# A message-passing kernel whose first table comes ahead of the check of dst, and whose last edges are cut into batches of 4, 4 and 1 tiles

## The chip, the core and the metric

The kernel runs on one core of a Trainium2 chip. A core has four compute engines, each with its own queue of instructions that it works off in order: TensorE (PE in the profile; PEld is its weight load), VectorE (DVE), ScalarE (ACT) and GpSimd (POOL). SyncE (SP) only issues DMAs here. Sixteen DMA engines move data between the chip's memory and the core's; SP and ScalarE feed one kind of queue (q1 and q10 in the profile), GpSimd another (q0). The metric is the device time of one execution in microseconds (us), lower is better.

## The reference

The graph has 1250 nodes with 512 values each and 40000 edges that are sorted by their target `dst`. One block of message passing is followed by a residual and a layer norm. Cut to what is computed:

```python
x_j = x[src]
v_j = x_j[:, :384].reshape(E, 128, 3)
s_j = silu(x_j[:, 384:] @ W1 + b1) @ W3 + b3
rbf = sqrt(2 / R_CUT) * sin(n * pi * r / R_CUT) / r          # n = 1..20, r = edge_weight
cutoff = 0.5 * (cos(pi * r / R_CUT) + 1) * (r < R_CUT)
s1, s2, s3 = thirds of s_j * (rbf * cutoff @ W2 + b2)
msg = concat([v_j * s1 + s3 * edge_attr, s2])
x1 = x + segment_sum(msg, dst)
x_j = x1[src]
v = x_j[:, :384].reshape(E, 3, 128) @ U ; v_V = v @ V
h = silu(concat([norm(v_V), x_j[:, 384:]]) @ Wu1 + bu1) @ Wu2 + bu2
s1, s2, s3 = thirds of h
msg = concat([v * s1, einsum(v, v_V) + s3])
out = layernorm(x + x1 + segment_sum(msg, dst))
```

## The kernel before

**What is computed per node instead of per edge.** `s_j` before the edge factor depends on the source node alone, so a first table of 10 blocks of 128 rows (L577, `table_row`) is written to memory once, and the edges gather rows of 640 values from it. The second message too depends on the source alone, so it is made once for each node, and the second segment sum becomes a product: `counts`, the number of edges from one node to another, times the rows of the second message. `counts` is gathered while the first message runs (`make_pair`, `mark_sources`, `count_links`).

**Tiling.** The edges are cut into 79 chunks of 512 (the last one holds 64), four chunks to a group, 20 groups. A batch is one tile of 128 edges from each of the four chunks of a group, so a group has four batches, and a batch is one step of the loop. The last group has three chunks, one with only 64 edges, so its batches have 3, 2, 2 and 2 tiles: 80 steps (`NT`). As `dst` is sorted, the edges of a chunk are expected to fall into a window of 32 target nodes that moves by 16 from chunk to chunk; L278 to L290 count the edges that do not (`missed`), and a branch at L383 takes `windowed` if there are none and `general` otherwise. With these inputs it is `windowed`.

**The front** (L126 to L385). The edge lists are loaded one chunk to a row by `load_edges` (L132): 78 full rows, and one more DMA for the 64 edges that are left. `dst` has a tile of its own; attributes, sources and weights lie in the memory of `counts`. SP issues in this order: dst, b3 and bu2, w1, b1, w3, weight, src, attributes, and later the ten stores of table rows. VectorE makes constants, then the check of `dst` (L278 to L290), then copies the transposed scalar part of the nodes (`turn_s`, L317). TensorE and ScalarE make the inner layer (`inner_layer`, L322 and L323), then each table row takes two matmuls (L336, L337), a ScalarE copy (L578), a VectorE product (L579) and a store on SP (L584). Between the rows the sources are turned (L344, L349), and behind them the second half of the bias is split into a high and a low part (`split_bias`, L360 to L365).

**The prologue of `windowed`** (L1458 to L1489). Weights and attributes are transposed (`by_tile`, L303 and L304, into `weight` and `carried`), VectorE makes `ratio` (L681), the arguments of the sines, `fade`, and the `basis` of the first group (L788), and then splits the sources (L699 to L721). ScalarE makes the sine (`turn`, L779). TensorE turns the basis (L800) and makes the edge factors `eb` of the first step (L854).

**The loop** (L1490). At each step VectorE makes the messages of a batch (`messages`: L812, L865, L883, L823, L869), TensorE adds those of the step before into the sums of a group (`add_messages`, L900 and L907) and counts its links (L925), then makes the edge factors of the next step into the one buffer `eb` (L854), which VectorE has to have read first. GpSimd gathers three steps ahead (`gather`, L745); the gathers are held behind `edge_factors` of the step by an explicit dependency. All other work is put into one of four lists, `first`, `early`, `late` and `dve`, by `at(when, step, rank, function)`, and runs at a fixed place of its step in order of rank:

```python
for t in range(max(*first, *early, *late, *dve) + 1):
    if t < NT:
        messages(t)
    run(first, t)
    if 1 <= t <= NT:
        add_messages(t - 1)
        count_links(t - 1)
    run(early, t)
    if t + 1 < NT:
        made = edge_factors(t + 1)
    if t + ahead < NT:
        gather(t + ahead, made)
    run(late, t)
    run(dve, t)
```

Such work is: closing a group (`close_group`, L938 to L951, the copies of the sums are L938 and L944), the counts (`low_counts` L960, `keep_counts` L969 and L974), and for each of ten blocks of nodes the sum of two groups (`sum_block`, L992, with a selection matrix `sel` that puts window rows to nodes), the nodes' own rows (`fetch_nodes` L999, `take_block` L1008), and the chain of the second message: `keep_rest` L1018, `turn_nodes` L1031, `times_u` L1042, `times_uv` L1058 with the squares L1062, `lengths` L1079, `root` L1096, `hidden` L1102, `curve` L1109, `factors` L1116 to L1132, `scale_row` L1138, `dot_row` L1147, `end_row` L1155 to L1164, `part_row` L1177. Block 8 takes sums of groups 16 and 17, block 9 those of 18 and 19.

**The tail.** Behind the messages the products of counts and rows (`products`, L1248) that were not made in the loop are made, the sums that were spilled are fetched and added on GpSimd (`add_begun`, L1221), the last counts are cast (`cast_counts`, L1231), and each block is added, normalised and stored (`end_out` L1279 to L1285, `norm_out` L1291 to L1303; the ten are done in `order`). The dependency on `ended` at L1236 keeps casts behind the last row of block 9.

Of the kernel before, what the change touches and what calls it, by code (L numbers as in the profile page):

```python
# [21 lines left out]
P = 128  # L22
C = 128
# [16 lines left out]
MARGIN = 8  # L40
WIN = SHARE + 2 * MARGIN
# [23 lines left out]
def gnn_resnorm(  # L65
# [63 lines left out]
    full = n_edges // CHUNK  # L129
    rest = n_edges - full * CHUNK  # L130

    def load_edges(t, ap, per=1):  # L132
# [10 lines left out]
    bias_f = front.tile([BIAS_ROWS - 1 + 32, V + 2 * C], F32, name="bias_f")  # L143
    nc.vector.memset(bias_f, 0.0)

    unfilled = full // 32 * 32
    nc.vector.memset(sh.att_r[unfilled:, :], 0.0)
# [8 lines left out]


    inside = SHARE * (NCP - 1) - MARGIN
    assert all(0 <= inside - (SHARE * c - MARGIN) < WIN for c in range(full, NCP))
    dst_r = front.tile([NCP, CHUNK], I32, name="dst_r")  # L160
    nc.gpsimd.memset(dst_r[unfilled:, :], inside)
    load_edges(dst_r, dst)
    first_last = slice(0, 3, 2)
    three = bias_f.rearrange("(r q) f -> r q f", q=32)[:, 0, :]
    nc.sync.dma_start(three[:, :V], b3.rearrange("(o f) -> o f", o=1).to_broadcast([3, V]))
    for h in range(2):
        nc.sync.dma_start(
            three[:, V + h * C : V + (h + 1) * C],
            bu2.rearrange("(h o c) -> h o c", o=1, c=C)[2 * h].to_broadcast([3, C]),
        )  # L170

    sh.nodes = const.tile([P, NB * width], F32, name="nodes")
    sh.xt = sh.nodes.rearrange("p (b f) -> p b f", f=width)
# [6 lines left out]
    last = n_nodes + MARGIN - (NB - 1) * P  # L180
    warm = const.tile([P, 1], F32, name="warm")
    nc.vector.memset(warm, 0.0)
    nc.vector.memset(sh.xt[last // 32 * 32 :, NB - 1, :], 0.0)
    nc.vector.memset(sh.xt[:MARGIN, 0, :], 0.0)

# [6 lines left out]
    load_all_nodes(nc.scalar, slice(V, width))  # L192

    nc.scalar.activation(warm, warm, AF.Silu)

    diff = front.tile([P, P], I32)
    nc.gpsimd.iota(diff, pattern=[[1, P]], base=0, channel_multiplier=-1)
    nc.gpsimd.memset(sh.src_r[unfilled:, :], 0.0)
# [6 lines left out]
    def load(engine, ap, shape, name):  # L205
        t = const.tile(shape, F32, name=name)
        engine.dma_start(t, ap)
        return t

    sh.h_t = const.tile([C, NB * P], F32, name="h_t")
# [1664 lines left out]
```

## Time and profile before

| | us |
|---|---|
| median of three runs | 591.55 |
| lowest and highest | 590.14, 593.16 |
| the profiled execution | 585.79 |
| its span, first to last instruction | 583.8 |

| engine | busy us | share |
|---|---|---|
| TensorE | 445.5 | 76% |
| VectorE | 441.8 | 76% |
| ScalarE | 373.6 | 64% |
| GpSimd | 354.5 | 61% |

The TensorE clock granted over the span is 0.888 of full speed. The profile is of one execution, so durations and waits in it add up to its own 583.8, not to the median. A line of a timeline is: start, duration, engine, line of the program, operation, the tile written and the one read, shapes, how often, and in brackets how long the engine was idle before and which instruction ended that.

Where the time lies: the first message starts at 41.04, a step of the loop takes some 6 to 6.5 from step 3 on, the last message ends at 539.77, and the last output is issued at 578.59. In the first 40 us the granted clock was 0.96 in 28 to 33 and 0.50 in 33 to 47.

### The profile page before, as it was taken

The numbers are of one execution on the slowest core, as the hardware profiler recorded it, in microseconds if no ns is written. First come the engines' busy times: TensorE is split into PE (matmuls) and PEld (weight loads), VectorE is DVE, ScalarE is ACT, GpSimd is POOL, SyncE is SP. The second block draws the span as 40 slices with busy tenths as digits, with TensorE's granted clock in tenths as the row PEclk, the third lists the DMA queues.
The fourth block names the chain that finished last, engine by engine and source line by source line (L and its number), as shares of the span: only waits on it lengthen the run. The fifth ranks groups of instructions, "written<-read, shape, count | busy, mean of one in ns | idle before, by whom it ended". The sixth has DMA issues, their size and how long they took to land. (4 is left out here: it accounts for less than half of the span.)

```text
span 583.8 us, 11028 instructions
## 1 busy us (share of the span) xinstructions
PE 445.5 (76%) x4193; PEld 240.2 (41%) x4193; DVE 441.8 (76%) x698; ACT 373.6 (64%) x941; POOL 354.5 (61%) x369
## 2 busy tenths in 40 slices
PE   2845667687777887697888786787777878798894
PEld 1422323344444344334435443443443444353673
DVE  7685867878878777878877777777787777687685
ACT  1455364757677665767776767777667778656455
POOL 7265767656667665656656665666666576643850
PEclk9966986888899777979888889998989899889998
DMA  8766777786777767767877777777777787859514
GB/s 240 257 189 213 200 224 216 210 262 200 216 224 243 228 197 218 214 205 220 253 245 201 253 226 213 233 231 242 220 229 224 218 240 224 241 148 285 210 38 146
DMA packets 38321, 126.95 MB, mean 217 GB/s; under 512 B 6688, under 2 KB 8238, under 8 KB 38258
## 3 DMA queue, kind: packets, MB, share of 16 engines
q0 software_dynamic: 26016, 104.86, 60.5%
q1 hardware_dynamic: 10910, 20.64, 10.2%
q10 hardware_dynamic: 1332, 0.64, 0.4%
q8 instruction: 35, 0.57, 0.4%
q14 instruction: 28, 0.23, 0.1%
HBM read 114.78 MB, written 11.34 MB: 216 GB/s over the span
## 5 line engine op out<-in xcount | busy, mean ns | idle before, releaser
L745 POOL DMA_INDIRECT more<-table,src_i x189 | 189.9, 1005 | 107.3 <-issue 44.0
L745 POOL DMA_INDIRECT nodes<-table,src_i x124 | 126.3, 1019 | 74.0 <-issue 28.3
L854 PE MATMUL eb<-w_sb,basis_t 25*128 25x388 f32 x626 | 83.5, 585 | 76.6 <-issue 42.2
L845 ACT ACTIVATE one<-one,weight,src_f 128x128 f16<-128x128 f16 x313 | 128.5, 482 | 0.5 <-issue 0.2
L835 ACT ACTIVATE one<-number,low 128x128 f16<-128x128 f16 x313 | 99.8, 392 | 8.5 <-PE adj L925 3.3
L812 DVE TENSOR_TENSOR hot<-lane,eb 128x128 f32<-128x128 f32 (+1 forms) x81 | 22.7, 281 | 81.6 <-PE eb L854 44.7
L869 DVE TENSOR_TENSOR more<-more,eb 128x1536 f32<-128x1536 f32 (+2 forms) x49 | 82.6, 1688 | 0.0
L854 PEld LDWEIGHTS eb<-w_sb,basis_t 25*128 25x128 f32 x626 | 27.5, 196 | 99.5 <-issue 58.0
L900 PE MATMUL agg<-more,hot 128*32 128x512 f32 (+1 forms) x378 | 66.0, 752 | 1.2 <-ACT sums L956 1.2
L865 DVE TENSOR_TENSOR more<-more,eb 128x1024 f32<-128x1024 f32 (+2 forms) x49 | 57.5, 1175 | 0.4 <-issue 0.3
L907 PEld LDWEIGHTS agg<-more,spread 128*32 128x32 f32 x1134 | 39.5, 125 | 40.8 <-issue 40.1
L869 DVE TENSOR_TENSOR nodes<-nodes,eb 128x1536 f32<-128x1536 f32 (+1 forms) x32 | 54.2, 1695 | 0.0
L907 PE MATMUL agg<-more,spread 128*32 128x128 f32 x1134 | 47.8, 298 | 0.0
L823 DVE TENSOR_TENSOR spread<-hot,eb 128x384 f32<-128x384 f32 (+1 forms) x81 | 43.0, 532 | 0.0
L925 PE MATMUL adj<-pair,one 128*128 128x160 f16 x313 | 37.9, 243 | 5.0 <-issue 4.9
L900 PE MATMUL agg<-nodes,hot 128*32 128x512 f32 x248 | 38.5, 680 | 2.4 <-ACT sums L956 2.4
L883 DVE TENSOR_TENSOR pair<-number,column 128x640 f16<-128x640 f16 (+1 forms) x81 | 38.5, 476 | 0.0
L805 ACT COPY basis_t<-work 128x512 f32<-128x512 f32 x20 | 11.7, 587 | 41.1 <-PE work L800 21.7
L865 DVE TENSOR_TENSOR nodes<-nodes,eb 128x1024 f32<-128x1024 f32 (+1 forms) x32 | 37.8, 1180 | 0.0
L960 DVE SCALAR_TENSOR_TENSOR both<-both,adj 128x400 f16<-128x400 f16 (+1 forms) x20 | 11.3, 566 | 32.0 <-ACT both L951 21.1
L907 PEld LDWEIGHTS agg<-nodes,spread 128*32 128x32 f32 x744 | 23.6, 116 | 23.1 <-issue 22.9
L925 PEld LDWEIGHTS <-one 128*128 128x128 f16 x313 | 20.8, 100 | 22.1 <-issue 20.7
(258 smaller groups left out, 728.8 us busy)
## 6 DMA issues: line engine op xcount, KB each, us to landing
table<-more SPq DMA_DIRECT2D x10, 320.0 KB
spilled<-begun SPq DMA_DIRECT2D x12, 256.0 KB
more<-table,src_i POOLq DMA_INDIRECT x189
more<-spilled SPq DMA_DIRECT2D x2, 1280.0 KB
resid<-h_t SPq DMA_DIRECT2D x9, 256.0 KB
node_x<-in_x_dram SPq DMA_DIRECT2D x8, 256.0 KB
nodes<-table,src_i POOLq DMA_INDIRECT x124
nodes<-in_x_dram POOLq DMA_DIRECT2D x2, 768.0 KB
```

The costliest lines, as they stand in the source:

```text
L745: got = nc.gpsimd.indirect_dma_start(out=rows_t[:n, j, :], out_offset=None, in_=sh.table1, in_offset=bass.IndirectOffsetOnAxis(ap=sh.src_i ...
L812: nc.vector.tensor_tensor(hots[t][:m, js, :], lane[:m, None, :WIN].to_broadcast(shape), eb[:m, js, V + 3 : V + 4].to_broadcast(shape), op= ...
L823: nc.vector.tensor_mul(spread[t][:m, js], hots[t][:m, js, None, :].to_broadcast(shape), eb[:m, js, V : V + 3, None].to_broadcast(shape),)
L835: nc.scalar.activation(onehots[t][:, j, :], number[:, :P], AF.Abs, bias=low[:, e : e + 1])
L845: nc.scalar.activation(one, one, AF.Relu, scale=less[:, e : e + 1], bias=worth[:, e : e + 1])
L854: made = nc.tensor.matmul(eb[:, j, : V + CARRY], turned[g][rows, i, :], sh.w2_sb[rows, :], start=True, stop=True,)
L865: nc.vector.tensor_mul(msg[:m, js, V:], msg[:m, js, V:], eb[:m, js, C:V])
L869: nc.vector.tensor_mul(msg[:m, js, :V].rearrange("p t (k c) -> p t k c", k=3), msg[:m, js, :V].rearrange("p t (k c) -> p t k c", k=3), eb[ ...
L883: nc.vector.tensor_tensor(pair[:m, js, :].rearrange("p t (l h) -> p t l h", h=2), number[:m, : PARTS * WIN].rearrange("p (l h) -> p l h", ...
L900: nc.tensor.matmul(agg[j * WIN : (j + 1) * WIN, :], hots[t][:m, j, :], msg[:m, j, :width], start=(i == 0), stop=False, skip_group_check=True,)
L907: nc.tensor.matmul(agg[j * WIN : (j + 1) * WIN, c * C : (c + 1) * C], spread[t][:m, j, c, :], msg[:m, j, width:], start=False, stop=(i == ...
L925: nc.tensor.matmul(to[:, :, at : at + WIN], one[:m, j, :], pair[:m, j, :].rearrange("e (p n) -> e p n", n=WIN), start=(i == 0 and j == js[ ...
```

## The change

*In the front* the loads are issued in another order (SP: w1, b1, b3, w3, dst, bu2, src, weight; the attributes only behind the ten stores of table rows). The copies of `turn_s` go from VectorE to ScalarE. The inner layer is cut into blocks (1, 2), (3, 4), (5 to 8), (0, 9), and the table rows of blocks 1 to 8 are made ahead of the check of dst, those of 0 and 9 behind its reduces and ahead of `missed`. The sources are turned behind row 8. One memset of a load's tile (`att_r`) goes from VectorE to GpSimd.

*The edges* are cut anew: 76 full chunks, and the last group has four chunks of 256, 256, 256 and 320 edges, so its batches have 4, 4 and 1 tiles (79 steps; 313 tiles before and after). Each edge list is therefore loaded as 76 rows, 4 half rows and one rest of 64. The windows of the last group's chunks lie in pairs on one another (`place_of`), so a second selection matrix `sel_last`, made on GpSimd, and one more matmul of 32 rows are needed for block 9.

*In the tail* the steps of block 8 come sooner, some additions on GpSimd and casts are put behind the last row, and the order of the outputs changes.

```diff
+    full = NCP - CPG
+    half = CHUNK // 2
+    odd = n_edges - full * CHUNK - CPG * half
+    sh.lengths = [half] * (CPG - 1) + [half + odd]
...
         nc.sync.dma_start(t[:full, :], flat[:n].rearrange("(c e) -> c e", e=CHUNK * per))
-        if rest:
-            nc.sync.dma_start(
-                t[full : full + 1, : rest * per], flat[n:].rearrange("(o e) -> o e", o=1)
-            )
+        m = n + CPG * half * per
+        nc.sync.dma_start(
+            t[full:NCP, : half * per], flat[n:m].rearrange("(c e) -> c e", e=half * per)
+        )
+        nc.sync.dma_start(
+            t[NCP - 1 : NCP, half * per : (half + odd) * per],
+            flat[m:].rearrange("(o e) -> o e", o=1),
+        )
...
+    sh.w1_sb = load(nc.sync, w1, [C, C], "w1_sb")
+    sh.b1_sb = load(nc.sync, b1.rearrange("(p o) -> p o", o=1), [C, 1], "b1_sb")
...
+    sh.w3_sb = load(nc.sync, w3, [C, V], "w3_sb")
+    load_edges(dst_r, dst)
...
+    load_edges(sh.src_r.bitcast(I32), src)
...
+    nc.gpsimd.memset(sh.att_r[unfilled:, :], 0.0)
+    load_edges(sh.wgt_r, edge_weight)
...
-    load_edges(sh.att_r, edge_attr, 3)
...
+        nc.scalar.copy(s_t[:, :n], tp[:, :n])
...
-        nc.vector.tensor_copy(s_t[:, : n * P], tp[:, : n * P])
...
+    first_s, next_s = turn_s((1, 2, 3, 4)), turn_s((5, 6, 7, 8))
+    inner_layer(first_s[:, : 2 * P], (1, 2))
+    inner_layer(first_s[:, 2 * P :], (3, 4))
+    part_bias(slice(0, V))
...
+    make_rows((1, 2))
+    inner_layer(next_s, (5, 6, 7, 8))
+    make_rows((3, 4, 5))
+    rest_s = turn_s((0, 9))
+    make_rows((6,))
+    inner_layer(rest_s, (0, 9))
+    make_rows((7, 8))
+
+
+    nc.vector.tensor_scalar(sh.src_r, sh.src_r.bitcast(I32), float(MARGIN), None, op0=ALU.add)
+    by_tile(ps_front, sh.src_r, 0, 1, sh.src_f, 1)
     local_r = front.tile([NCP, CHUNK], F32)
     nc.vector.tensor_scalar(local_r, dst_r, share, None, op0=ALU.subtract)
     ends = front.tile([NCP, 2], F32)
...
+    make_rows((0, 9))
     nc.tensor.matmul(missed, misses, ones[:NCP, 0:1], start=True, stop=True)
     nc.vector.tensor_copy(missed_i, missed)
...
+    nc.vector.tensor_copy(sh.src_i, sh.src_f)
+    load_edges(sh.att_r, edge_attr, 3)
     by_tile(ps_front, local_r, 0, 1, sh.local, 1)
...
+    at = half // P * CPG + CPG - 1
+    nc.vector.memset(sh.local[odd:, NGR - 1, at : at + 1], NOWHERE)
+    nc.vector.tensor_scalar(w2_sb[:, V:], lane[:, :CARRY], own, None, op0=ALU.is_equal)
+    part_bias(slice(V, V + 2 * C))
...
+    sh.sel_last = const.tile([P, P], F32, name="sel_last")
+    nc.gpsimd.tensor_scalar(sh.sel_last, lane, place_last, None, op0=ALU.is_equal)
...
+    def place_of(g, j):
+
+        return (j if g < NGR - 1 else j // 2) * SHARE
...
         def close_group(g):
-            agg, rows = aggs.pop(g), group_rows(g)
+            agg = aggs.pop(g)
...
+                sums[g] = pool.tile([P, width], F32, name="sums_1", bufs=2)
+                nc.scalar.copy(sums[g], agg)
...
+            sel = sh.sel_last if (b, k) == (NB - 1, 1) else sh.sel[:, k, :]
+            nc.tensor.matmul(blks[b], sel, sums.pop(2 * b + k), start=(k == 0), stop=(k == 1))
+            if (b, k) == (NB - 1, 0):
+                over = slice(P - WIN, P)
+                nc.tensor.matmul(
+                    blks[b], sh.sel[over, 1, :], sums[2 * b + 1][over, :], start=False, stop=False
+                )
...
-                nc.vector.memset(node_x[rows // 32 * 32 :, :], 0.0)
+                nc.gpsimd.memset(node_x[rows // 32 * 32 :, :], 0.0)
...
+                if b == NB - 2:
+                    links_at = (
+                        (dve, 1, 1, take_block), (dve, 2, 3, keep_rest), (late, 2, 6, turn_nodes),
+                        (early, 3, 1, times_u), (late, 3, 1, times_uv), (late, 4, 1, lengths),
+                        (first, 5, 3, root), (late, 5, 1, hidden), (first, 6, 1, curve),
+                        (late, 6, 1, factors), (dve, 6, 1, scale_row), (dve, 6, 3, dot_row),
+                    )
+                    last = (first, 7, 1)
             else:
-                at(late, begin - 2, 9, sum_block, b, 0)
+                at(late, begin - 1, 9, sum_block, b, 0)
                 at(late, begin, 1, sum_block, b, 1)
...
-        for step, bs in ((NT, (0, 1)), (NT + 1, (2, 3, 4)), (NT + 2, (5, 6, 7))):
+        for step, bs in ((NT, (0, 1)), (NT + 1, (2, 3, 4))):
             at(dve, step, 10, add_begun, bs)
+        at(first, ends[NB - 1], 8, add_begun, (5, 6))
+        at(first, ends[NB - 1], 10, add_begun, (7,))
...
-                gather(t + ahead, made)
+                gather(t + ahead, made if t + ahead < NT - 2 else None)
...
-        order = (0, 4, 5, 6, 3, 1, 2, ACCS, ACCS + 1, old)
+        order = (0, 4, 3, 1, 5, 6, 2, ACCS, ACCS + 1, old)
```

More of the change, by code (lines that the diff above doesn't have):

```diff
@@ L1235, in cast_counts @@
                 cast = copy(to[:, n : n + m, :], view)
[L1236 to L1240 removed]
+                behind_rows(cast)
                 for k in range(m):
```

309 lines of the change are left out of this document (152 added, 157 removed).

## The prediction

> **What bounds the kernel now.** I read the page first (busy shares, groups of instructions), then the timelines of the first 45 us and of the last 65 us engine by engine, then three windows of the DMA view. All times are microseconds from the start of the span of the profiled execution: 583.8 of span and 2.0 around it make its 585.79.
>
> No engine is full over the whole span. The groups say what paces the loop: VectorE waits for the edge factors in front of most of its 81 steps, and TensorE makes these factors into one buffer that VectorE's last message instruction (L869) frees.
>
> ```profile
> PE 445.5 (76%) x4193; PEld 240.2 (41%) x4193; DVE 441.8 (76%) x698; ACT 373.6 (64%) x941; POOL 354.5 (61%) x369
> L812 DVE TENSOR_TENSOR hot<-lane,eb 128x128 f32<-128x128 f32 (+1 forms) x81 | 22.7, 281 | 81.6 <-PE eb L854 44.7
> L869 DVE TENSOR_TENSOR more<-more,eb 128x1536 f32<-128x1536 f32 (+2 forms) x49 | 82.6, 1688 | 0.0
> ```
>
> The change leaves steps 1 to 73 alone, so only two stretches count: what comes ahead of the first L812, and what comes behind step 75. In the front VectorE's timeline reads (start, duration, in brackets the idle time before and what ended it):
>
> ```profile
> 9.76 0.14 DVE L290 CAST missed_i<-missed 1x1 int32<-1x1 f32 x1 [0.28 <-PE missed L289]
> 19.62 3.12 DVE L579 TENSOR_TENSOR more<-nodes,pp 128x384 f32<-128x384 f32 x4 [1.46 <-ACT more L578]
> 26.82 1.47 DVE L579 TENSOR_TENSOR more<-nodes,pp 128x384 f32<-128x384 f32 x2 [0.19 <-ACT more L578]
> 30.88 0.36 DVE L681 TENSOR_SCALAR ratio<-weight 128x320 f32<-128x320 f32 x1 [0.87 <-DVE bias L365]
> 36.30 0.69 DVE L788 TENSOR_TENSOR basis<-turn,fade 128x320 f32<-128x320 f32 x1
> 41.04 0.29 DVE L812 TENSOR_TENSOR hot<-lane,eb 128x128 f32<-128x128 f32 x1
> ```
>
> The ten table rows start at 19.62 and end at 28.29, the second half of the bias follows, then the branch at L383, then from 30.88 a chain without a gap: 5.42 to the basis, 4.74 to the first message. ScalarE runs beside it, and its order matters: the three copies of the edge attributes come ahead of the sine that the basis reads.
>
> ```profile
> 31.82 1.27 ACT L304 COPY carried<-tp 128x320 f32<-128x320 f32 x2
> 33.40 0.70 ACT L304 COPY carried<-tp 128x320 f32<-128x320 f32 x1 [0.32 <-PE tp L303]
> 33.90 0.46 ACT L779 ACTIVATE turn<-turn 128x320 f32<-128x320 f32 x1
> ```
>
> In the tail the last messages run in batches of 3, 2, 2, 2 tiles; the chain goes through one stall of VectorE, then the last sum (L992), the last block's rows, and products that TensorE works off nearly without a gap until 575.28. The end is theirs:
>
> ```profile
> 529.67 0.55 DVE L1079 TENSOR_REDUCE s<-square 128x128 f32<-128x384 f32 x1 [2.87 <-ACT square L1062]
> 537.66 0.22 DVE L812 TENSOR_TENSOR hot<-lane,eb 128x64 f32<-128x64 f32 x1 [1.05 <-PE eb L854]
> 575.56 0.67 DVE L1279 TENSOR_TENSOR h_t<-h_t,adj 128x512 f32<-128x512 f32 x1
> ```
> ```profile
> 543.65 1.13 PE L992 MATMUL begun<-sums,sel 128*128 128x512 f32 x2 [0.46 <-ACT sums L944]
> 546.80 0.66 PE L1031 MATMUL work<-ident,x 128*128 128x128 f32 x4 [0.75 <-DVE x L1164]
> 574.88 0.40 PE L1248 MATMUL adj<-lower,cast_last 128*128 128x512 f32 x1
> ```
>
> **The front, step by step.** After the change ScalarE is the first to be ready: its table load ends at 7.50 and the warm-up at 7.72. Then one copy of s_t (0.69, as VectorE's at L317), a layer over two blocks (half of a cold layer: four instructions of L322 took 3.75 for two layers, so 0.94), its silu (0.47, the shorter form of L323), and from the row's first matmul to VectorE's part 2.13 (17.49 to 19.62): about 11.5 to 12, where it was 19.62. VectorE's setup and the check (5.0 to 9.5) no longer stand ahead of it. A row takes 0.82 when TensorE is warm (L336 starts 19.01, 19.83, 20.64) and about twice that cold (1.52 from 17.49 to 19.01). With three cold and five warm, row eight ends at 11.5 + 4.6 + 4.1 = 20.2; all warm 18.1, all cold 24. Behind it now come the source add (0.41, L344), the check (0.48 for L278, 1.35 for two reduces, 0.30 for two small ones) and the last two rows (1.47), together 4.0: last row at 24.3, against 28.29. Then the missed copy 0.14, the source cast 0.31, a short memset 0.06, w_sb 0.23 and the second bias half 1.81 (28.21 to 30.02), 2.6 in all: 26.9, with the 0.86 of the branch 27.8, against 30.88. VectorE's own path would gain 3.1 (bounds 2 to 4.5 from the two clocks). The 16x1536 memset goes from VectorE to GpSimd, and seven small operations are added there; GpSimd is idle for 10.7 ahead of L655, so they cost nothing unless they reach the branch.
>
> **The attribute load is what I see as going wrong.** It was issued at 11.83 and had landed long before its transposes at 29.77. Now it stands on SP behind the ten table stores, the last of which can be issued only after the last row: 24.3 + 0.4, and the store itself takes 2.0 (the last row ended at 28.29, the stores' traffic at about 30.3). So its data begin to move at about 26.0. How long they take depends on how its rows are dealt out:
>
> ```profile
> q1 hardware_dynamic: 108, 0.20, 81.0%
> ...
> q1 hardware_dynamic: 42, 0.23, 87.8%
> ...
> q1 hardware_dynamic: 166, 0.38, 99.1%
> ```
>
> These are SP's queue in three windows of one microsecond (packets, MB, share of 16 engines): at 13 and 14.5 it carries loads of 78 rows, at 26 stores of 128 rows. 81.0% is 13 of 16, and 13 is the largest number up to 16 that divides 78; 128 rows fill 16. The second share is above 13/16, so this is an inference and no proof. If it holds, the change's 76 rows (4 times 19) go to 4 engines. The middle window moved 0.23 MB in a microsecond, 17.7 KB per engine with 13 engines; 456 KB on 4 engines would then take 114/17.7 = 6.4, where 13 need about 2.0. So the load lands at 28.0 to 28.7 if it is spread (2.0 to 2.7), at 32.4 if it is not, and later when gathers, which start at about 30.3, share these 4 engines. From the landing it is one set of transposes (0.6) and the copies (31.82 to 34.10), 2.9, and the sine 0.46 to the basis: spread, 32.1, ahead of VectorE's own 27.8 + 5.4 = 33.2, so nothing is late; on 4 engines 35.8 to 38.8 (the upper end: from 30.3 on the gathers take half of each engine, and 2.1 that remain take 4.2, with the last row also 0.8 later), against 36.30 before. I take 36.7, between the ends but nearer to the undisturbed one: the front gives -0.4, bounds -2.5 to +1.3 (the lower end with the last row 0.8 sooner). VectorE's 4.74 behind the basis is not moved ahead of it, so this lands on the first message in full. The dst, source and weight loads have the same 76 rows (38 KB per engine, 2.1 each), but are issued in the first 6 us and first read at about 20.
>
> The Trainium skill, "DMA: Bandwidth & Descriptors", section "Why a DMA increments its semaphore by 16 and not by 1", states that a transfer is spread over the largest number up to 16 which divides the slowest dimension of both sides: 13 for 78 rows, 4 for 76. By it the load takes the longer way; if the rows were dealt out evenly whatever their count, the sum would be the early rival's below.
>
> **The tail, step by step.** One step goes (80 to 79). The node update of block 8 starts two steps sooner, so the stall of 2.87 moves from between steps 76 and 77 to between 75 and 76. From L812 of step 75 (517.77): step 75 takes 5.04 as before plus a stall of 2.7, step 76 with four tiles 5.5 (four-tile steps just before took 5.6 to 5.9), step 77 4.5 (3.95 of messages and the small work behind), the single tile 1.5 (a two-tile batch took 2.11): messages end at 537.0, against 539.77. Behind that came 5.03 to the end of L992 at 544.8. Now the 32-row matmul added in the last block's sum takes up to 1.0 (as the pair in L992), and ScalarE has its two table loads (1.28 each, L1096 and L1109) packed into steps 77 and 78: 0.6 more. So the sum ends at 543.6, 1.2 sooner; of TensorE's gaps of 0.75 and 0.40 behind it about half goes, because block 8's last work (L1079, L960, L1164: 1.3) no longer stands between that sum and L1031. The tail gives 1.7; bounds 0 (ScalarE's chain takes all of it) and 4.0 (2.8 of messages and both gaps). Behind that nothing is removed: the products and the ten normalisations at 1.58 keep their length. The GpSimd adds moved behind the last rows (nine of about 1.44) leave VectorE's two-operand instructions faster (L1138 took 1.35 beside them, 0.56 without), but products fill TensorE meanwhile. fetch_nodes' memset leaves VectorE (0.48), inside a step that waits for factors.
>
> **Sum.** 585.79 + 0.4 - 1.7 = 584.5 in the profiled execution. That one lies 5.8 under the median of the runs shown (591.55); with the same shift the median becomes 590.2.
>
> **The rivals.**
> - *As forecast:* the attributes come late, the tail gives a little: 590.2. The two terms lie up to 2.1 and 1.7 from their bad bounds and 1.7 and 2.3 from their good ones; as roots of summed squares 587.3 to 592.9. Chance 0.47.
> - *The attributes come in time* (rows dealt over 13 or more engines): front 3.1, tail 1.7, 586.8, in the same way 584.1 to 588.8. For it: the second window's 87.8% is above 13/16. Against it: 81.0%. Chance 0.22.
> - *Slower, gathers crowd the load:* of the 6.4 about 2.1 remain when the gathers start. In a late window where both queues were busy (534 to 535) the gathers had 54.8% and SP's queue 35.4%, 1.55 to 1. At that ratio 2.1 take 5.4, the basis comes at 39.1, and with the tail's 1.7 it is 592.6. At three to one the rest takes 8.4, the basis comes at 42.1, and the time is 595.7. It decides from a basis at about 41, that is attributes landing at 37.6. Against it: with few gathers in flight at the start the queue isn't full. Chance 0.17.
> - *The tail gives nothing:* ScalarE's chain for block 8 in fewer, fuller steps makes a second stall (L1138 already waited 0.77 for L1132), and the front is the forecast's: 592, with 590.5 to 595. Chance 0.14.
>
> **How the numbers follow.** About 0.5%, 3.0, is what a measurement of this kernel can tell from no change: under 588.6 counts as faster, over 594.5 as slower. Faster: 0.20 from the second case, 0.14 from the low end of the first, 0.01 from the last: 0.35. Slower: 0.14 from the crowded load, 0.04 from the last case, 0.03 from the first: 0.21. The rest is 0.44. The range, 585.3 to 595.0, takes in the early case and most of the crowded one and leaves out some 0.15; the likeliest case's own is 587.3 to 592.9.
>
> **What would show it.** Right: the first L579 at about 11 to 12 and the last row at 23.5 to 25.5; SP's queue at a share near 25% for some 6 us after the table stores; VectorE idle ahead of the basis, with the attribute copies as releaser, and the basis at 35.8 to 38.8; in the tail the stall one step sooner and the last sum's end 1 to 2 us sooner. Wrong: the load at 13 or 16 engines' share and a basis at 33 (then 586.8), or a stall longer than 3 us in steps 76 to 78.

## The result, and the profile after

Medians of 20 runs each: 600.09 us after the change (593.4 to 604.97), 592.58 before (587.69 to 599.98). The ratio is 1.0112, with a 95% interval of 1.0079 to 1.0144: 6.6 us slower, clear of no change though a difference of about 1%, where 1.4 us faster was forecast. The profiled execution after the change has a span of 597.6, 13.8 more than the one before; but the one before lies 6.8 under its median and the one after 0.7, so about half of that difference is only between executions.

The page after, the same groups as before (engine, line, operation, count, then busy time and mean ns, then idle time ahead and what ended most of it):

```profile
PE 453.2 (76%) x4197; PEld 246.1 (41%) x4197; DVE 436.9 (73%) x687; ACT 375.3 (63%) x945; POOL 359.5 (60%) x379
L837 DVE TENSOR_TENSOR hot<-lane,eb 128x128 f32<-128x128 f32 (+1 forms) x79 | 22.5, 285 | 90.1 <-PE eb L879 49.5
L894 DVE TENSOR_TENSOR more<-more,eb 128x1536 f32<-128x1536 f32 x48 | 83.9, 1747 | 0.0
```

VectorE does 5 us less work (436.9 against 441.8), and its idle time ahead of the first message instruction of a step has grown by 8.5 (90.1 against 81.6). So the loss is in waits. In the front, VectorE's timeline after:

```profile
11.69 0.66 DVE L607 TENSOR_TENSOR more<-nodes,pp 128x384 f32<-128x384 f32 x1 [1.04 <-ACT more L606]
...
23.20 1.27 DVE L607 TENSOR_TENSOR more<-nodes,pp 128x384 f32<-128x384 f32 x2
...
27.31 0.33 DVE L706 TENSOR_SCALAR ratio<-weight 128x320 f32<-128x320 f32 x1 [0.49 <-DVE bias L310]
...
37.64 0.69 DVE L813 TENSOR_TENSOR basis<-turn,fade 128x320 f32<-128x320 f32 x1 [5.17 <-ACT carried L274]
...
43.09 0.29 DVE L837 TENSOR_TENSOR hot<-lane,eb 128x128 f32<-128x128 f32 x1 [0.71 <-PE eb L879]
```

The rows start 7.9 earlier and the branch's other side begins 3.6 earlier, and then VectorE stands still for 5.17 ahead of the basis. TensorE's line tells why, and SP's queue (packets, MB, share of 16 engines, here for the microsecond from 28) tells what it waited for:

```profile
34.25 1.30 PE L273 MATMUL tp<-ident,counts 80*128 80x80 f32 x8 [8.10 <-DMA counts<-in_edge_attr_dram]
```
```profile
q1 hardware_dynamic: 16, 0.10, 24.5%
```

The attributes have come 8.10 after TensorE was free for them, at a quarter of 16 engines. The first message starts 2.05 later than before (43.09 against 41.04). Much of that does not last: before, the third step began 9.68 after the second, after the change 6.04, and by step 12 the changed kernel is 0.5 ahead (117.88 against 118.35).

The tail is where most of the time in the profile went. Before, step 74 began at 511.84 and step 75 at 517.77:

```profile
511.84 0.29 DVE L812 TENSOR_TENSOR hot<-lane,eb 128x128 f32<-128x128 f32 x1 [0.44 <-PE eb L854]
517.77 0.29 DVE L812 TENSOR_TENSOR hot<-lane,eb 128x128 f32<-128x128 f32 x1 [0.99 <-PE eb L854]
```

After the change, VectorE's timeline reads so, with TensorE's and GpSimd's below it:

```profile
515.74 0.29 DVE L837 TENSOR_TENSOR hot<-lane,eb 128x128 f32<-128x128 f32 x1 [0.44 <-PE begun L1286]
...
529.02 0.29 DVE L837 TENSOR_TENSOR hot<-lane,eb 128x128 f32<-128x128 f32 x1 [7.75 <-PE begun L1286]
...
538.39 0.55 DVE L1113 TENSOR_REDUCE s<-square 128x128 f32<-128x384 f32 x1 [5.02 <-ACT square L1096]
...
550.64 0.19 DVE L837 TENSOR_TENSOR hot<-lane,eb 128x32 f32<-128x32 f32 x1 [0.22 <-PE eb L879]
...
588.68 0.67 DVE L1317 TENSOR_TENSOR h_t<-h_t,adj 128x512 f32<-128x512 f32 x1
```
```profile
519.75 0.93 PE L879 MATMUL eb<-w_sb,basis_t 25*128 25x388 f32 x8 [0.65 <-DVE nodes L894]
526.43 1.12 PE L1065 MATMUL work<-ident,x 128*128 128x128 f32 x4 [5.75 <-issue]
...
558.27 1.12 PE L1023 MATMUL begun<-sums,sel_last 128*128 128x512 f32 x2 [0.50 <-ACT sums L967]
```
```profile
515.98 0.94 POOL L770 DMA_INDIRECT more<-table,src_i  x1 [1.83 <-PE begun L1286]
...
521.21 0.95 POOL L770 DMA_INDIRECT more<-table,src_i  x1 [0.30 <-issue]
...
526.22 0.95 POOL L770 DMA_INDIRECT nodes<-table,src_i  x1 [0.30 <-remote]
```

Step 75 begins 13.28 after step 74 (529.02 against 515.74; 5.93 before), step 76 another 9.84 after that (5.04 before). During the first of these waits GpSimd issues nine gathers one behind the other, 0.3 apart, since those of the last two batches no longer wait for edge_factors (the hold, below). TensorE's line says that the factors of step 75 were started at 519.75 and took 0.93, which would have freed VectorE at 520.7. But a matmul's end in such a line is modelled. A semaphore is a counter by which an engine tells the others that an instruction is done, and the trace's records of it show when TensorE's count truly rose, beside the first landing of each gather, as far as landings are on record:

```
TensorE's count rises:   519.55  520.32  521.75  523.21  524.62  526.05  528.18
first landing of a gather:       520.38  521.80  523.25  524.63  526.15
```

TensorE's completions came in small groups with the landings, 1.43 apart. ScalarE's copy at 526.11 and VectorE at 529.02 followed them at once. So the work was issued in time and finished late, while gathers ran.

From the first message instruction of step 74 to the end the changed kernel takes 81.9, the kernel before 72.0. That is 9.9 of the 13.8. All of that lies ahead of the end of the last sum (L1023, L992 before), which comes 43.7 after the start of step 74, against 32.9; from there to the end the changed kernel takes 38.2, the kernel before 39.0. The clock granted to TensorE differs too: 0.83 from step 74 to the end, 0.95 before. The trailing does not come from it: the clock was 1.00 from 512 to 521.9, where the first three rises of the list lie (from 522 to 535 it was 0.50). But a part of the tail's loss may be the clock's, and no run takes the two apart. Another 4.4 is in steps 12 to 73, which the change leaves alone (392.2 against 387.9; the runs below have 384 to 393 there).

### The profile page after: what moved, and what is told of

Same layout as the page of the kernel before. It is cut to its first block, busy times and chain, and to the rows that moved or that the text cites. A ratio compares the mean times of both kernels' runs of the same rounds, so it can differ in the third digit from the quotient of the medians.

```text
span 597.6 us, 11058 instructions
## 1 busy us (share of the span) xinstructions
PE 453.2 (76%) x4197; PEld 246.1 (41%) x4197; DVE 436.9 (73%) x687; ACT 375.3 (63%) x945; POOL 359.5 (60%) x379
## 4 chain that ended last, share of the span: by engine, by line
PE 55%; DVE 25%; issue 10%; ACT 5%; POOL 2%; DMA 2%; DVEq 0%; another core or an unknown queue 0%; ACTq 0%; POOLq 0%
PE eb L879 17%; PE agg L925 9%; PE agg L932 6%; DVE more L894 5%; DVE more L890 4%; PE begun L1286 4%; DVE nodes L894 4%; PE work L1023 4%; DVE spread L848 3%; PE adj L950 3%; DVE pair L908 3%; DVE nodes L890 3%; PE work L1108 2%; PE work L825 2%; DMA nodes<-in_x_dram 2%
## 5 line engine op out<-in xcount | busy, mean ns | idle before, releaser
L770 POOL DMA_INDIRECT more<-table,src_i x192 | 194.0, 1010 | 109.7 <-issue 44.2
L770 POOL DMA_INDIRECT nodes<-table,src_i x121 | 123.6, 1022 | 70.8 <-issue 27.8
L879 PE MATMUL eb<-w_sb,basis_t 25*128 25x388 f32 x626 | 85.7, 585 | 75.8 <-DVE more L894 30.6
L837 DVE TENSOR_TENSOR hot<-lane,eb 128x128 f32<-128x128 f32 (+1 forms) x79 | 22.5, 285 | 90.1 <-PE eb L879 49.5
L894 DVE TENSOR_TENSOR more<-more,eb 128x1536 f32<-128x1536 f32 x48 | 83.9, 1747 | 0.0
L925 PE MATMUL agg<-more,hot 128*32 128x512 f32 x384 | 66.7, 763 | 2.3 <-ACT sums L978 2.3
L890 DVE TENSOR_TENSOR more<-more,eb 128x1024 f32<-128x1024 f32 x48 | 58.3, 1215 | 0.3 <-issue 0.3
L932 PEld LDWEIGHTS agg<-more,spread 128*32 128x32 f32 x1152 | 41.2, 128 | 40.0 <-issue 38.3
L925 PE MATMUL agg<-nodes,hot 128*32 128x512 f32 x242 | 40.9, 721 | 2.2 <-ACT sums L978 2.2
L932 PEld LDWEIGHTS agg<-nodes,spread 128*32 128x32 f32 x726 | 26.5, 126 | 23.5 <-issue 22.7
L932 PE MATMUL agg<-nodes,spread 128*32 128x128 f32 x726 | 31.7, 304 | 0.0
```

The source lines that it names most:

```text
L770: got = nc.gpsimd.indirect_dma_start(out=rows_t[:n, j, :], out_offset=None, in_=sh.table1, in_offset=bass.IndirectOffsetOnAxis(ap=sh.src_i ...
L879: made = nc.tensor.matmul(eb[:, j, : V + CARRY], turned[g][rows, i, :], sh.w2_sb[rows, :], start=True, stop=True,)
L890: nc.vector.tensor_mul(msg[:m, js, V:], msg[:m, js, V:], eb[:m, js, C:V])
L894: nc.vector.tensor_mul(msg[:m, js, :V].rearrange("p t (k c) -> p t k c", k=3), msg[:m, js, :V].rearrange("p t (k c) -> p t k c", k=3), eb[ ...
L925: nc.tensor.matmul(agg[j * WIN : (j + 1) * WIN, :], hots[t][:m, j, :], msg[:m, j, :width], start=(i == 0), stop=False, skip_group_check=True,)
L932: nc.tensor.matmul(agg[j * WIN : (j + 1) * WIN, c * C : (c + 1) * C], spread[t][:m, j, c, :], msg[:m, j, width:], start=False, stop=(i == ...
```

## The experiments

The runs fell on chips of two kinds. On one, as in the pair above, the kernel before takes 580 to 592; on the other it takes 499 to 500. The granted clock over the span differs as well (0.86 to 0.90, and 0.93 to 0.96), and each chip was used at one time only, so "kind of chip" may be a state that a chip was in. Ratios are to the kernel before on the same chip. Their intervals don't cover a change of chip: e11 and e16 below are one kernel, and their intervals don't meet. All of the differences are under 2%. "Step" rows of the tables are differences of the start of a step's first message instruction.

**The kind of chip of the case, first four runs.**

`e1_held`, the gathers held again:

```diff
-                gather(t + ahead, made if t + ahead < NT - 2 else None)
+                gather(t + ahead, made)
```

> The changed kernel with one thing undone: the gathers of the last two batches wait for edge_factors again. In the changed kernel VectorE sat idle for 7.75 us ahead of L837 at 529.02, while nine gathers ran back to back and TensorE's completions came only with their landings. Theory G (the gathers that aren't held stop TensorE): that idle time falls below 2 us, and the ratio to the kernel before falls from 1.011 to 0.998 to 1.002 (about -7 us). Theory P (block 8's earlier steps make the stall): it stays at 5 us or more in the same step and the ratio stays at 1.008 to 1.014. Theory R (that stall is a chance of one execution): no such stall here, and the ratio stays at 1.008 to 1.014 all the same.

`e2_block8_old`, block 8's steps at their old places:

```diff
-                if b == NB - 2:
-                    links_at = (
...
-                    last = (first, 7, 1)
...
-                for step in (3, 6) if b < NB - 1 else (2, 6):
+                for step in (4, 8) if b < NB - 1 else (2, 6):
```

> The changed kernel with block 8's steps at their old places (links_at, last, and the two steps of add_parts as before); the gathers aren't held. Theory G: the long wait of VectorE ahead of L837 in step 75 stays, 5 us or more, and the ratio to the kernel before stays within 1.006 to 1.014. Theory P: the wait goes, and the ratio falls to 0.998 to 1.004.

`e3_before_unheld`, the kernel before with the change's hold:

```diff
-                gather(t + ahead, made)
+                gather(t + ahead, made if t + ahead < NT - 2 else None)
```

> The kernel before with one thing added: the gathers of its last two batches (2 tiles each) don't wait for edge_factors. Theory G: they run straight behind those of the batch ahead, VectorE gets a wait of 2 to 6 us ahead of an L812 in steps 76 to 78 that it didn't have, and the ratio to the kernel before is 1.003 to 1.010. Theory P and theory R: no new wait, ratio 0.997 to 1.003.

`e4_attr16`, the changed kernel with its loads in rows that 16 divides, and a rest:

```diff
-        nc.sync.dma_start(t[:full, :], flat[:n].rearrange("(c e) -> c e", e=CHUNK * per))
+        rows = flat[:n].rearrange("(c e) -> c e", e=CHUNK * per)
+        for first, end in by_sixteen(full):
+            nc.sync.dma_start(t[first:end, :], rows[first:end, :])
```

> The changed kernel with each load of 76 rows issued as one of 64 and one of 12 rows. If rows are dealt out over the largest number up to 16 that divides them (theory K), 64 rows go over 16 engines and 12 over 12: the attribute load's share of SP's queue is near 90% for about 2 us in place of 25% for some 6, VectorE's idle time ahead of the basis falls from 5.17 us to under 1, and the basis starts at about 33 instead of 37.64. The ratio then falls by at most 0.008, and by less than 0.003 if the first steps of the loop wait for gathers anyway. If rows are dealt out evenly whatever their number, nothing changes: basis at 37 to 38.

**Then, on another chip of this kind.** `e5_front_only` is the kernel before with the change's front and loads of 64 and 14 rows; `e6_held_attr16` puts the edits of e1 and e4 together; `e7_held_attr16_block8` adds that of e2; `e8_before_again` is the kernel before, unaltered.

> The kernel before with the change's front alone (rows ahead of the check, new order of loads, attributes behind the table stores), its old cut of the edges and its old tail; the loads of 78 rows go as 64 and 14. Theory F (the front is worth something once the attributes come in time; what is lost is lost in the tail): first message at 38.5 to 40, step 12 at 113 to 115 against 118 before, ratio to the kernel before 0.990 to 0.996. Rival (the loop's first steps wait for gathers or for TensorE and eat what the front gains): ratio 0.997 to 1.003.

> The changed kernel with the gathers held again and the loads split into 64 and 12 rows. If both costs are separate and add up (1.011 with neither; each alone gave 1.008 and 1.003), the ratio is 0.996 to 1.001; no wait over 2 us ahead of L839 in step 75. If they overlap, 1.001 to 1.004. By theory F the tail from the first message instruction of step 74 to the end still takes 75 to 78, against 72 before.

> As the run with the gathers held and the loads split, with block 8's steps at their old places too. Theory S (the early steps of block 8 put VectorE's reduce behind ScalarE's squares while gathers slow TensorE, and cost 3 to 4): VectorE's wait ahead of L1113 (10.7 us for step 75 to 76 with the gathers held) goes, steps 74 to 78 get 2 to 4 shorter, and the ratio is 0.003 to 0.006 lower than with the new places. Rival (the old places only move the wait behind the last message): the last message comes sooner, the last sum and the end don't; ratio equal or higher.

> The kernel before once more, for a second profile: which of its numbers repeat. Expected: first message 39.5 to 41.5, step 2 at 56 to 58 (the stall in step 1 recurs), from L812 of step 74 to the end 71 to 74, and 382 to 390 for steps 12 to 73.

What was measured, in us of each profile:

| kernel | ratio (95%) | first message | step 12 | 12 to 73 | 74 to 75 | 75 to 76 | 74 to end |
|---|---|---|---|---|---|---|---|
| before | | 41.04 | 118.35 | 387.9 | 5.93 | 5.04 | 72.0 |
| e8, before again | | 39.73 | 116.93 | 384.0 | 5.08 | 5.04 | 71.8 |
| after | 1.0112 (1.0079 to 1.0144) | 43.09 | 117.88 | 392.2 | 13.28 | 9.84 | 81.9 |
| e1, held | 1.0079 (1.0048 to 1.0111) | 43.85 | 116.54 | 384.7 | 6.49 | 10.69 | 77.3 |
| e2, block 8 old | 1.0171 (1.0123 to 1.0218) | 47.64 | 120.39 | 387.0 | 10.32 | 6.42 | 80.6 |
| e3, before unheld | 1.0045 (1.0001 to 1.0088) | 39.78 | 117.65 | 387.2 | 5.08 | 9.00 | 75.6 |
| e4, loads split | 1.0027 (0.9990 to 1.0063) | 39.21 | 113.66 | 388.6 | 13.08 | 9.53 | 81.6 |
| e5, front only | 0.9943 (0.9913 to 0.9973) | 39.15 | 114.17 | 385.7 | 5.11 | 5.04 | 73.7 |
| e6, held and split | 0.9958 (0.9922 to 0.9995) | 41.66 | 114.63 | 387.1 | 6.58 | 10.70 | 75.0 |
| e7, and block 8 old | 1.0036 (1.0002 to 1.0071) | 39.40 | 113.59 | 392.9 | 6.55 | 7.84 | 77.3 |

*The hold.* Without it step 75 begins 13.3, 10.3 and 13.1 after step 74, with it 6.5 to 6.6 in three profiles; block 8's places make no such difference (e2). The start of step 75 in e1, with a wait of 0.94 in place of 7.75, and the stall that is left behind it:

```profile
513.01 0.29 DVE L837 TENSOR_TENSOR hot<-lane,eb 128x128 f32<-128x128 f32 x1 [0.94 <-PE eb L879]
...
523.23 0.55 DVE L1113 TENSOR_REDUCE s<-square 128x128 f32<-128x384 f32 x1 [6.27 <-ACT square L1096]
```

Put into the kernel before, the missing hold makes a wait that was not there, in step 75, where the last two batches' four gathers now run (from 518.39; in the kernel before the first of them starts at 523.05, in step 76):

```profile
524.38 0.31 DVE L812 TENSOR_TENSOR hot<-lane,eb 128x64 f32<-128x64 f32 x2 [5.05 <-PE agg L907]
```

That line is of e3: 9.00 from step 75 to 76, against 5.04 in both profiles of the kernel before, and the granted clock was 1.00 throughout. Theory G stands as to the wait, the chance of one execution (R) and block 8's places (P) fall. Its size in time is smaller than in the step, and than theory G forecast (0.998 to 1.002 for e1, which gave 1.0079): the tail gets 5.6 shorter (76.2 as the mean of e1 and e6, 81.8 of after and e4), while the ratio fell by 0.0033 from after to e1 and by 0.0069 from e4 to e6, so 2 to 4 us. Each pair is of two chips and its intervals overlap, so the ratios alone don't show it. The granted clock in the tail was 0.83 and 0.84 without the hold, 0.88 and 0.89 with it (after and e4; e1 and e6), so a part of the 5.6 may be the clock's. e2's 1.0171 is above what either theory forecast; its step 12 came late (120.39), and the rest is not explained.

*The attributes.* With 64 and 12 rows (e4) SP's queue has this for the microsecond from 27, and VectorE's basis this:

```profile
q1 hardware_dynamic: 51, 0.25, 86.2%
```
```profile
33.63 0.69 DVE L815 TENSOR_TENSOR basis<-turn,fade 128x320 f32<-128x320 f32 x1 [1.46 <-ACT turn L806]
```

The share goes from 24.5% to 86.2%, the bytes of a microsecond from 0.10 to 0.25 MB, the wait from 5.17 to 1.46 (under 1 was expected), and the basis from 37.64 to 33.63. Unlike the first step's 2.05 this lasts: step 12 begins at 113.6 to 114.6 in the four kernels with split loads, at 116.5 to 120.4 in the three with 76 rows, and at 116.9 to 118.4 in the three with the old front. So by step 12 the front with split loads is worth some 3.6 (a mean of 114.0 against 117.6), and with 76 rows nothing. By the ratios (after and e4; e1 and e6, again of two chips each) the split is worth 0.0085 and 0.0121, or 5 to 7 us, more than I expected of it; where the rest of that lies the profiles don't show. The edit splits the loads of dst, sources and weights too, so a part may be theirs.

*Block 8.* Theory S falls. The old places do take the long step 75 to 76 away (7.84 against 10.70), but the last sum ends 36.4 after the start of step 74 (547.95 less 511.59) against 36.1 (543.36 less 507.30), the end comes 2.3 later, and the ratio is 0.0078 higher. As the rival said, the wait only moves (in e7 step 76 takes 7.31, in e6 5.07).

*What is best.* e5 and e6 are both faster than the kernel before on this kind of chip, 0.9943 and 0.9958, with intervals that stay below 1; the two overlap. The front with split loads carries the gain in both, and the change's new cut and tail add nothing that these runs can tell (the tail 75.0 against 73.7).

**Two more on the way of the attributes, and the hold in the whole loop.** All four fell on a chip of the other kind. `e12_held_attr_early` is e1 with the attributes, 76 rows in one piece, issued right behind the weights and so ahead of the table stores:

```diff
     load_edges(sh.wgt_r, edge_weight)
+    load_edges(sh.att_r, edge_attr, 3)
...
-    load_edges(sh.att_r, edge_attr, 3)
```

> The changed kernel with the gathers held and the attribute load, still 76 rows in one piece, issued right behind the weights and so ahead of all table stores. Theory K (it is the slow load behind the stores, not the slow load alone): the attributes land by 25, the basis comes at 32 to 33.5, and the ratio is 0.993 to 0.999, as with the loads split (0.9958). If the slow load holds the table stores up on its four engines, the first gather starts later than 31 and the ratio is 1.000 to 1.006.

The ratio was 1.0117 (1.0076 to 1.0159). The basis came at 32.28, as theory K has it, and the rival came true all the same; GpSimd and VectorE of e12:

```profile
35.96 1.10 POOL L770 DMA_INDIRECT more<-table,src_i  x1 [7.17 <-DMA node_x<-in_x_dram]
```
```profile
43.90 1.22 DVE L890 TENSOR_TENSOR more<-more,eb 128x1024 f32<-128x1024 f32 x1 [6.43 <-DMA more<-table,src_i]
```

The first gather starts at 35.96 (29.97 after the change) and VectorE then waits 6.43 for its rows. The stores stand behind the slow load in the queue, and the gathers behind the stores. To issue this load earlier was no cure; the ratio is worse than the rival's 1.000 to 1.006.

`e11_front_attr8` is e5 with the attributes ahead of the last two stores, `e10_all_unheld` the kernel before with no hold at all, and `e9_half_rows` the changed kernel with half of each row in the last three batches' gathers:

```diff
+    load_edges(sh.att_r, edge_attr, 3)
     make_rows((0, 9))
...
-    load_edges(sh.att_r, edge_attr, 3)
```
```diff
-                gather(t + ahead, made)
+                gather(t + ahead)
```
```diff
+                h = 1 if t < NT - 3 else 2
...
-                    out=rows_t[:n, j, :],
+                    out=rows_t[:n, j, : (V + 2 * C) // h],
...
-                    in_=sh.table1,
+                    in_=sh.table1 if h == 1 else sh.table1.rearrange("n (h f) -> (n h) f", h=h),
```

> The kernel before with the change's front, loads split, as in e5_front_only (0.9943), and the attribute load issued ahead of the stores of the last two table rows. VectorE then waits less than 0.3 ahead of the basis, which comes at 32 to 32.5 in place of 33.24; the last two stores come some 2 us later, and with them the first gather. If the first steps wait for the basis, the ratio is 0.991 to 0.994; if for the gathers, 0.994 to 0.999.

> The kernel before with no gather held behind edge_factors: only free rooms and POOL's own order hold them. Theory G (gathers that run while TensorE adds messages slow it) says that the loop's steps get longer: 6.4 to 6.9 per step from step 12 to 73 in place of 6.2 to 6.3, ratio 1.02 to 1.08. If it is only the end of the loop that is sensitive, the ratio is 1.000 to 1.008, since in the loop free rooms hold the gathers anyway.

> The changed kernel, its gathers not held; the gathers of the last three batches bring 320 of 640 values per row (from the wrong half rows: this part of the sums is not the reference's), with as many descriptors as before. In the changed kernel TensorE's completions in step 74 came one group with each landing, 1.43 us apart, and step 75 began 13.28 after step 74 (13.08 with the loads split). If the moved bytes slow TensorE (theory B), landings come every 0.8 to 1.25 us and the step falls to 8 to 10.5. If the number of descriptors or of gather instructions does it (theory D), it stays at 12 to 13.5.

e11 gave 0.9871 (0.9784 to 0.9958), on two runs alone; its basis came at 32.56 without a wait and its first gather at 31.70 (29.10 in e5), as expected. e10 gave 0.9929 (0.9887 to 0.9971); e9's step 75 began 5.46 after step 74, and so says nothing of bytes or descriptors. On this chip most steps of the loop take 5.0 to 5.1, VectorE is busy nearly throughout (47.7 of the 50 us from 200 in e12), and TensorE's count rises at the modelled ends while gathers run (in e12 the spread matmuls that the model ends at 406.06 to 406.50 raised the count at 406.06 to 406.57; after the change, on the other kind, such a set that the model ends at 460.52 to 460.98 raised it from 460.54 to 463.5; the granted clock was 1.00 in both places).

**Repeats.**

> As e9_half_rows (the changed kernel, gathers not held, the last three batches bring half of each row; this part of the sums is not the reference's), which fell on a chip where the kernel before takes 500 and TensorE's completions don't trail behind gathers. On a chip where the kernel before takes 580 to 592: if the moved bytes slow TensorE (theory B), step 75 begins 8 to 10.5 after step 74, against 13.28 and 13.08 with whole rows; if the number of descriptors or of gather instructions does it (theory D), 12 to 13.5. On a chip that takes 500 the run tells nothing more: 5.0 to 5.5.

> As e10_all_unheld (the kernel before, no gather held), which gave 0.993 where the kernel before takes 500. On a chip where it takes 580 to 592, theory G expects longer steps, 6.4 to 6.9 from step 12 to 73, ratio 1.01 to 1.05; if only the end of the loop is sensitive, 0.996 to 1.006.

> The changed kernel once more, unaltered. On a chip where the kernel before takes 580 to 592: ratio 1.008 to 1.014, step 75 begins 10 to 14 after step 74, first message at 42 to 48. On a chip where it takes 500: step 75 begins 5 to 6 after step 74, and the ratio is 1.000 to 1.009 (the attributes late, the gathers' part gone).

> As e11_front_attr8 (the kernel before with the change's front, loads split, attributes issued ahead of the last two stores), whose interval of 0.978 to 0.996 told little. If the first steps wait for the basis, 0.989 to 0.993; if for the gathers, 0.994 to 0.999, no better than with the attributes behind all stores (0.9943).

> The kernel before, for a profile on a chip of the kind on which it takes 500 (where e9 to e16 fell). There the changed kernel had its first message at 43.10, L812's counterpart of step 12 at 105.28, 318.2 from step 12 to 73 and 69.9 from step 74 to the end. If the late attributes alone make its 1.0115 there, the kernel before has step 12 at 100 to 102 and the tail within 2 of 70 to 73; if the loop does, 312 to 315 for steps 12 to 73. On a chip of the other kind: first message 39.5 to 41.5, tail 71 to 74 once more.

> The changed kernel with the gathers held and the loads split into 64 and 12 rows, as e6_held_attr16 (0.9958, 0.9922 to 0.9995). On a chip of the kind that takes 500: the front gives what the attributes cost (first message at 38 to 40, step 12 at 101 to 102.5), ratio 0.996 to 1.005. On the other kind: 0.992 to 1.000 again.

These too fell on chips of the kind that takes 500:

| kernel | ratio (95%) | first message | step 12 | 12 to 73 | 74 to 75 | 74 to end |
|---|---|---|---|---|---|---|
| e17, before | | 40.26 | 103.11 | 318.8 | 5.08 | 73.0 |
| e15, after | 1.0115 (1.0044 to 1.0186) | 43.10 | 105.28 | 318.2 | 5.45 | 69.9 |
| e18, held and split | 1.0010 (0.9971 to 1.0048) | 39.23 | 102.19 | 318.2 | 5.46 | 70.4 |
| e16, front, attributes sooner | 1.0041 (1.0008 to 1.0074) | 37.60 | 101.60 | 318.2 | 5.07 | 73.5 |
| e14, before, none held | 0.9974 (0.9928 to 1.0020) | 40.58 | 103.62 | 311.3 | 5.07 | 75.4 |

There the wait in step 74 is gone without the hold (5.45), as G must have it where TensorE does not trail, and the change's tail is 3.1 shorter than the old one. The front with the late attributes costs 2.2 at step 12, where e18, with the loads split, gains 0.9. For the changed kernel the 3.1 and the 2.2 give a gain of 1, but the ratio of e15 (four runs) is a loss, as large as on the other kind of chip though the wait in step 74 is gone, and e18's is none. e16's is a loss too, where 0.989 to 0.999 had been expected, although each stage of its profile is equal or shorter, except the tail by 0.5. What makes up these ratios on this kind of chip is not settled: one profile of each kernel does not show it. e13 (5.57 from step 74 to 75) again tells nothing of the cause, and theory G's longer steps without any hold (e10, e14) stay untested, as that forecast was for the other kind of chip.

## Why the prediction was wrong

**The tail's sum failed: it took step 74 as unchanged and gave the missing hold no cost.** It counts from L812 of step 75 on, and has no term for `made if t + ahead < NT - 2 else None`, though that line is in the diff and acts from step 74 on. Step 74 took 13.28, against 5.93 before: 7.4 of the 9.9. The edit only takes a wait away from GpSimd, so I gave it no cost; but that wait kept gathers off TensorE's heels. With it step 74 takes 6.5 (e1, e6), and the tail is 5.6 shorter.

Inside the sum the stall was mis-sized. Step 75 was put at 7.7, "5.04 as before plus a stall of 2.7", steps 76 and 77 at 5.5 and 4.5, and all from step 75 to the end of the messages at 19.2, with a gain of 1.7 for the tail. They took 9.84, 5.81, 5.97 and 23.3, and the tail lost 9.9. The stall came where it was put, between steps 75 and 76, but was 5.0, and 6.3 with the hold (L1113 in e1, L1115 in e6, both for ScalarE's squares, which wait for TensorE): five gathers are issued in that step of e1, from 513.25 to 518.47, and TensorE's count trails there too. The old places are no better, which speaks for the fuller step and against the order as its cause; no run shows the fuller step alone.

This is not the whole loss. On the chips that take 500 the changed kernel lost as much (1.0115 in e15) with a step 74 of 5.45, and nothing with the loads split (1.0010 in e18, whose gathers are held too, but there with no effect on step 74: 5.46).

**The front was read rightly in its mechanism; its size is open.** The first row was put at 11.5 to 12 (11.69), the last at 24.3 (24.47), the restart behind the branch at 27.8 (27.31), SP's share near 25% (24.5%), the basis at 36.7 in a range of 35.8 to 38.8 (37.64). The sum's front term was -0.4; the first message came 2.05 later, but step 12 begins 0.5 sooner, so by the profiles what lasts is about nothing, as forecast. By the ratios it is a loss of some 2 to 4 (an estimate: 0.0085 to 0.0121 for the 76 rows less the 0.0057 that e5 gains, of 590); which of the two holds is not settled. What hid the 2.05 was not in the working: the kernel before loses some 4 between its second and third steps (9.68, 10.18 in e8), and the changed kernel does not. Two readings in the working were off. Its terms for the start of the load, 24.3, 0.4 and 2.0, add up to 26.7 and not 26.0, and the transposes that waited for the load began at 34.25, where the landing had been put at 32.4. And the 81 is the count of L812's instructions; the loop has 80 steps.

The rule of the Trainium skill on which that part was weighed ("DMA: Bandwidth & Descriptors", "Why a DMA increments its semaphore by 16 and not by 1") has rows dealt over the largest number up to 16 that divides them: 4 for 76 rows, 16 for 64. The trace agrees: 24.5% against 86.2% of the engines.

**The rivals.** "The attributes come in time" is what e4 made of the kernel, and it shows that the rival's 3.1 for the front was about right (3.6). "Gathers crowd the load" happened once in part: in e2 the basis came at 38.92 and the first message at 47.64; but it was not what made the change slower. "The tail gives nothing" looked at the right stretch, at too small a price: its second stall, VectorE's for ScalarE's factors, is there (1.67 at L1172 after the change, 4.17 in e1, 0.77 before), but the larger waits are for TensorE in steps 74 and 75.

The Trainium skill, "SBUF — State Buffer", section "Who interferes with whom", says that DMA does not contend with compute engines and that TensorE waits on no one. Of the ports that it speaks of no run here tells anything. On the chips that take 500 the trace agrees that TensorE does not trail; on the chips that take 580 to 592 it does not agree, with completions 1.43 apart in the rhythm of landings. There the measurement decides, though what TensorE waits for there no run shows.

## What to carry to other kernels

A wait in a queue that looks like pure delay may be what keeps two engines out of each other's way: before it is taken out, price it from a step where the two overlap. A load's row count is part of its cost: here 64 and 12 rows moved 0.25 MB in a microsecond, 76 rows 0.10. And where an engine seems to wait for work that the timeline ended long ago, compare the modelled end with the semaphore's own times.

## What the runs showed of the hardware

TensorE's matmuls were finished some 8 us after their modelled end while gathers were in flight (factors of step 75: 520.7 modelled, 528.2 to 529.0 by the count). It is not any DMA traffic: in the kernel before, where loads from SP filled the engines just as much, in the microsecond from 539, the counts rose at the modelled ends.

```profile
q1 hardware_dynamic: 204, 0.42, 107.1%
```

And it is not every chip: on some the same kernel shows no such trailing and takes 500 in place of 590, with a loop step of 5.2 in place of 6.3 on average (steps 12 to 73 of e17 and e8). Whether it is the gathers' bytes, their descriptors or their issue was to be told by e9 and e13; as no chip of the trailing kind came up for them, it stays open. On the chips without it the hold costs: with no gather held the loop is 7.5 shorter (311.3 in e14 against 318.8 in e17), of which the tail takes back 2.4; the ratios are 0.9929 and 0.9974, and the second one's interval takes in 1.
